# A planned transformer block on one core: w1 in two early loads, block 0's LayerNorm in halves, another order of the first seven products, and turned tokens that go through DRAM

## The chip, the core and the metric

One core of one Trainium2 chip runs the kernel. The core has TensorE (PE; its weight loads are shown as PEld), VectorE (DVE), ScalarE (ACT), GpSimd (POOL) and the queue of SyncE (SP), from which nearly all transfers (DMA) are issued. Each engine works off its own instructions in the order in which they were written, and waits at an instruction until the semaphores that it names have come. The metric is the device time of a run in microseconds (us); the median of the runs of one chip counts.

## The reference

The kernel computes one conditioned block of a sequence model on x of 2 x 2048 x 512 numbers in fp32:

```
emb = silu(t) @ ada_w + ada_b                   # t: 2 x 512, ada_w: 512 x 3072
shift1, scale1, gate1, shift2, scale2, gate2 = split(emb, 6)
norm = layernorm(x) * (1 + scale1) + shift1
h    = gelu(norm @ w1 + b1)                     # w1: 512 x 512
x    = x + gate1 * (h @ w2 + b2)                # w2: 512 x 512
norm = layernorm(x) * (1 + scale2) + shift2
hf   = gelu_tanh(norm @ fw1 + fb1)              # fw1: 512 x 1024
out  = x + gate2 * (hf @ fw2 + fb2)             # fw2: 1024 x 512
```

All numbers are fp32. The six parts of emb are called groups 0 to 5 in the code (mods 0 and 1 are shift1 and scale1, 2 is gate1).

## The kernel before, in words

**Tiling.** The 4096 tokens are eight blocks of 512 (NBLK = 8; four per batch row). A block lies as 128 partitions x 4 slots (C = 4) x 512 features. The work has two stages: for each block `ssm1` (norm @ w1, Gelu) and `ssm2` (h @ w2, added to x; the result x1 is also stored to DRAM), and then, for pairs of blocks, `ff1` and `ff2`. The first stage takes the span's first third, about to 190 us.

**Seven products.** Each matrix product is done with seven half-size products in place of eight (a Strassen form with carried sums): operands are cut in quarters, `first` and `second` (lines 362 and following) form sums of quarters on VectorE and POOL, and P1 to P7 run on TensorE. In `ssm1` a product is four matmuls of 128x256. Products share three banks: P1, P6, P7 and P4 write bank y, P2 bank x, P5 and P3 bank v. In the order CARRIED (P1, P5, P6, P2, P7, P3, P4) ScalarE copies P1's bank to bank x, so that P2 adds to it; P6 adds to P1 in bank y and is taken out by two ScalarE activations (Identity with bias), after which P7 goes on in the same bank. P2's result gets a Gelu, the first one of the kernel, ahead of which the compiler places a table load on ScalarE.

**Turning tokens.** A product needs features on partitions. For block i from 2 on, `norm1` (L562) loads x, takes the statistics on VectorE (`stats`), the scale on POOL (`scales`), normalizes on ScalarE and transposes squares of 32x32 on VectorE (L530) into one of two block buffers (`blocks`, in the tile far). `move` (L556) then brings sixteen pieces of 32 partitions x 512 (64 KB) to their partitions in the tile turned, one transfer each; ScalarE applies shift and scale (`modulate`), and VectorE or POOL form the sums. Blocks 0 and 1 are turned by TensorE (`turn_rows`, matmuls with an identity at L296). `norm2` does the same for the second LayerNorm through DRAM: four transfers of 256 KB out (`turned_d`), and four back in `ff1`'s `tokens`.

**The start.** `small_loads` brings biases and the condition on ScalarE's queue. SP's queue holds x of block 0 (two halves), ada_w's groups 0 and 1, w1 and group 2 (1 MB each), and small loads of gate biases (`load_gate_b`, 1 KB each) where the planner puts them. TensorE runs warm-up products with the identity (`warm`), the two modulations (`modulation`: 16 matmuls, a transpose and an add on VectorE), block 0's turning, and then `ssm1(0)`. Of block 0 the statistics, the scale and the normalizing are done for all four slots at once.

**What sets the order.** `Plan` records every operation with its engines, its cost and its latency. `order` gives each a due time from the order of TensorE's matmuls, which is the program's, and `simulate` plays the queues with these costs and writes out the order that comes of it. Of a transfer it knows the issue, a pipe with a rate, and a landing. So a change of a cost or of one operation can move instructions on VectorE, ScalarE, POOL and SP through the whole program. The framework gives transfers eight semaphores in turn, so that a transfer waits for the eighth before it to land; the planner before does not know of this.

Of the kernel before, what the change touches and what calls it, by code (L numbers as in the profile page):

```python
# [16 lines left out]
class Op:  # L17
    __slots__ = ("n", "engs", "fn", "cost", "lat", "shared", "size", "lead", "care", "after", "done", "deps", "succ", "late", "on", "start", "end", "note")


class Plan:
# [9 lines left out]
    RATED, LANDED = 0.5, 4000.0  # L31
    LITTLE = 1 << 15
    AHEAD, SLACK = 2500.0, 150.0

# [29 lines left out]
    def add(self, engs, fn, outs, ins, cost, lat, shared="", size=0, lead=0.0):  # L64
        op = Op()
        op.n, op.engs, op.fn, op.cost, op.lat, op.shared, op.size = len(self.ops), engs, fn, cost, lat, shared, size
        op.deps, op.succ, op.note, op.lead, op.care = set(), [], self.stage, lead, self.care
        op.after, op.done = None, None
# [12 lines left out]
        self.ops.append(op)  # L81
        return op

    def order(self):
# [11 lines left out]
        for _ in range(2):  # L96
            for op in reversed(ops):
                late = due.get(op.n, 1e9)
                for s in op.succ:
                    late = min(late, ops[s].late - (1 + op.care) * (self.HOP + min(op.lat.values()) + op.size / self.RATE))  # L100
                op.late = late
            self.simulate()
            wait = ops[self.anchor].start - due[self.anchor]
            due = {n: t + wait for n, t in due.items()}
        return sorted(ops, key=lambda op: (op.start, op.n))

    def simulate(self):
# [5 lines left out]
        at, pools, found = 0, {e: [] for e in "vags"}, {}  # L113
        done = [False] * len(ops)

# [8 lines left out]
        def choose(e):  # L124
# [23 lines left out]
        while count:  # L148
# [42 lines left out]
def kernel(  # L191
# [110 lines left out]

    def dma(o, a, q="s", lead=0.0, lat=2000.0):
# [4 lines left out]
        plan.add(q, lambda E: E.dma_start(out=o, in_=a), outs, ins, {q: plan.ISSUE}, {q: lat}, size=size, lead=lead)  # L308

    def memset(o, value):  # L310
# [40 lines left out]

    x1_d = [far(f"x1_{i}", P, C, D) for i in range(NBLK)]
    turned_d = {i: far(f"turned_{i}", P, C, D) for i in SOON}
    fw1_d = far("fw1_parts", 7, P, 7, W)
# [66 lines left out]
    def load_x(i, pieces=1, xs=xs):  # L421
        for s in range(pieces):
            c = slice(s * C // pieces, (s + 1) * C // pieces)
            dma(xs[i][:, c], x_blk[i][:, c])

    def load_ada(g):
        dma(ada_t[g], ada_w[:, g * D : (g + 1) * D].rearrange("(k p) n -> p k n", p=P))

# [54 lines left out]

    def stats(xt):
# [8 lines left out]

    def scales(t, mv, v="g"):
        ve, r, e, rstd, nmr = [t[:, 32 + C * n : 32 + C * (n + 1)] for n in range(5)]
        var, mean = mv[:, :, 1], mv[:, :, 0]
        small("g", lambda E: E.tensor_scalar(ve, var, 1.0, EPS, ALU.mult, ALU.add), ve, [var])
        small("g", lambda E: E.tensor_tensor(r, ve, half_t, ALU.pow), r, [ve, half_t], 1090)  # L498
        if v == "v":
# [4 lines left out]
        else:  # L504
# [5 lines left out]
            small(v, lambda E: E.tensor_scalar(nmr, nmr, -1.0, None, ALU.mult), nmr, [nmr])  # L510
        return rstd, nmr

# [28 lines left out]

    def norm1_sums(i):
        h = cut(turned[i], "p a (k h r) -> p a k h r", k=KD, h=2)
        lo, hi = h[:, :, :2], h[:, :, 2:]
        q = {"11": lo[:, :, :, 0], "12": lo[:, :, :, 1], "21": hi[:, :, :, 0], "22": hi[:, :, :, 1]}
        return second(q, thirds(turned_s[i]))

# [13 lines left out]

    def norm1(i, queues="s"):  # L562
# [7 lines left out]
    def turn_rows(i, xn, k, bank, e):  # L570
        for c in range(C):
            turn_by_pe(banks[bank][:, c * P : (c + 1) * P], xn[:, c, k * P : (k + 1) * P], ident, c == 0, c == C - 1)
        o = turned[i][:, :, k * P : (k + 1) * P].rearrange("p a (c q) -> p a c q", c=C)
        a = cut(banks[bank], "p (c a q) -> p a c q", c=C, a=C)
        shift, scale = mods[0][:, k, :1], mods[1][:, k, :1]
        if e == "v":
            plan.add(
                "v",
                lambda E: E.tensor_scalar(o, a, scale, shift, ALU.mult, ALU.add),
                [o],  # L580
                [a, scale, shift],
                {"v": 600},
                {"v": 690},
            )
        else:
            act(o, a, AF.Identity, shift, scale)

    def rows_normed(i):
# [9 lines left out]
    def norm2(i):  # L598
        plan.stage = f"norm2 {i}"
        bl = normed(xs[i], xs[i], next_blocks())  # L600
        for a in range(C):
            dma(turned_d[i][:, a].rearrange("(m q) r -> q m r", m=C), bl[a * G : (a + 1) * G])

# [28 lines left out]
    def ssm1(i, ops, wops, hooks={}):  # L632
        plan.stage = f"ssm1 {i}"
# [3 lines left out]
        s1, u2, s5 = lo[:, :, :HT], lo[:, :, HT:], hi[:, :, HT:]  # L637
        for n, p in enumerate(CARRIED):
            product(
# [402 lines left out]
    load_ada(0)  # L1042
    load_ada(1)
    load_w(w1_t, w1)
    load_ada(2)
# [21 lines left out]

    t0, mv0 = stats(xs[0])
    plan.add("v", lambda E: E.tensor_copy(cols_t[:, :ROWS], banks[1][:, :ROWS]), [cols_t[:, :ROWS]], [banks[1][:, :ROWS]], {"v": 130}, {"v": 200})
# [9 lines left out]
    plan.add("v", lambda E: E.tensor_copy(picks, pick), [picks], [ident], {"v": 560}, {"v": 640})  # L1079
    rstd0, nmr0 = scales(t0, mv0, "v")  # L1080
    w1q = {"11": w1_t[:, :2, : D // 2], "12": w1_t[:, 2:, : D // 2], "21": w1_t[:, :2, D // 2 :], "22": w1_t[:, 2:, D // 2 :]}
    modulation(0, 1)
    warm((7,) * 3, 2)
    xn = cut(blocks[1], "p (c d) -> p c d", c=C)
    for c in range(C):
        normal(xn, xs[0], c, rstd0, nmr0, "av"[c % 2])
    modulation(1, 2)
# [8 lines left out]
    def turn_first():  # L1096
        plan.stage = "norm1 1"
        for k in range(2):
            turn_rows(1, xn1, k, 1 + k, "a")

    def turn_second():
        plan.stage = "norm1 1"
        for k in range(2, 4):
            turn_rows(1, xn1, k, k - 1, "a")
        tok[1] = norm1_sums(1)
# [4 lines left out]
    plan.anchor = len(plan.ops)  # L1110
    hid = {0: ssm1(0, tok[0], w1_ops, {"P2": lambda: gate_rows_of(2, 1), "P3": first_weight2})}
    w2_ops = gated[0]
# [88 lines left out]
```

## Time and profile before

| what | us |
|---|---|
| median of three runs (579.44, 579.64, 582.99) | 579.64 |
| the profiled execution | 580.96 |
| its span, first to last instruction | 579.2 |
| TensorE busy in the span | 567.2 |
| VectorE, ScalarE, POOL busy | 462.2, 240.2, 319.0 |

The mean granted clock of TensorE is 0.996. In a row of a timeline the columns are start, length, engine, line, operation, tile written and tiles read, shapes, count; in brackets the idle time ahead of it and what ended it. Names ending in q (SPq) are a queue's issue of a transfer. The busy time of TensorE is modelled at the ends of matmuls. Buffer numbers are left out: far, for one, holds block buffers, block 0's x and the identity.

### The profile page before, as it was taken

What the parts mean: (1) busy time and instruction counts of PE and PEld (TensorE: products, weight loads), DVE (VectorE), ACT (ScalarE), POOL (GpSimd) and SP (SyncE); (2) the same over time, 40 slices, a digit from 0 to 9 for tenths busy, and PEclk for the clock granted to TensorE, in tenths of its full rate; (3) what the DMA queues carried; (4) which work ended last, traced back from release to release, by engine and by line L of the source; (5) the groups of instructions that cost most, each with busy time, mean ns of one, the idle gap of its engine ahead of it and who ended that gap; (6) DMA issues with size and microseconds to landing.
All of it is one profiled execution on the core that took longest, in us unless ns stands there. A gap on an engine that the chain in (4) does not pass through costs nothing.

```text
span 579.2 us, 9609 instructions
## 1 busy us (share of the span) xinstructions
PE 567.2 (98%) x3307; PEld 505.6 (87%) x3307; DVE 462.2 (80%) x872; ACT 240.2 (41%) x414; POOL 319.0 (55%) x404
## 2 busy tenths in 40 slices
PE   8999999999998999999999999999999999999997
PEld 5788888888787888888999888999888999888997
DVE  5695865889696688889896789888889997789846
ACT  2463955656384644665202265102255211235010
POOL 1695344889680598976810436711897544336620
PEclk9999999999999999999999999999999999999999
DMA  8953576789578995895034755056846043520022
GB/s 299 392 220 80 185 197 186 220 309 321 175 245 229 346 358 183 314 308 172 30 118 144 236 162 194 23 142 230 296 158 218 1 145 115 195 91 1 2 74 72
DMA packets 49867, 106.96 MB, mean 185 GB/s; under 512 B 6000, under 2 KB 10012, under 8 KB 48924
## 3 DMA queue, kind: packets, MB, share of 16 engines
q1 hardware_dynamic: 49744, 106.34, 55.8%
q8 instruction: 26, 0.43, 0.3%
q14 instruction: 21, 0.17, 0.1%
q10 hardware_dynamic: 76, 0.02, 0.0%
HBM read 68.45 MB, written 31.60 MB: 173 GB/s over the span
## 4 chain that ended last, share of the span: by engine, by line
PE 85%; DMA 5%; POOL 3%; DVE 2%; SPq 2%; issue 1%; ACT 1%; DVEq 0%; ACTq 0%; POOLq 0%
PE bank L286 84%; SPq L308 2%; DMA turned<-far 2%; DMA fw<-in_L_cond_ada_w_dram 1%; DMA ring<-in_L_cond_ssm_w_dram 1%; DMA fw_parts<-fw 1%; POOL near L248 1%; POOL hidden L248 1%; DVE far L530 1%; ACT turned L266 1%; DVE turned L248 0%; POOL fw L248 0%; ACT hidden L266 0%; POOL marks L498 0%; ACT bank L275 0%
## 5 line engine op out<-in xcount | busy, mean ns | idle before, releaser
L286 PE MATMUL bank<-turned,ring 128*128 128x256 f32 x896 | 206.0, 381 | 1.6 <-DMA ring<-in_L_cond_ssm_w_dram 1.3
L286 PEld LDWEIGHTS bank<-turned,ring 128*128 128x128 f32 x896 | 170.2, 191 | 26.3 <-ACT turned L266 1.5
L248 DVE TENSOR_TENSOR hidden<-bank,hidden 128x512 f32<-128x512 f32 (+2 forms) x170 | 125.0, 757 | 41.1 <-PE bank L286 37.4
L248 DVE TENSOR_TENSOR rows<-bank,rows 128x256 f32<-128x256 f32 (+3 forms) x234 | 99.1, 456 | 26.3 <-PE bank L286 19.8
L286 PE MATMUL bank<-near,hidden 128*128 128x256 f32 x448 | 99.9, 382 | 3.8 <-DVE far L248 2.1
L286 PEld LDWEIGHTS bank<-near,hidden 128*128 128x128 f32 x448 | 84.6, 190 | 17.1 <-DVE far L248 2.5
L286 PE MATMUL bank<-ring 128*128 128x256 f32 x336 | 82.2, 381 | 0.0
L286 PE MATMUL bank<-fw,hidden 128*128 128x128 f32 (+1 forms) x512 | 80.1, 301 | 0.0
L286 PEld LDWEIGHTS bank<-fw,hidden 128*128 128x128 f32 x512 | 72.9, 191 | 3.9
L275 ACT COPY bank<-bank 128x512 f32<-128x512 f32 (+2 forms) x67 | 32.3, 482 | 101.4 <-PE bank L286 100.8
L286 PEld LDWEIGHTS bank<-ring 128*128 128x128 f32 x336 | 63.2, 190 | 10.6 <-ACT bank L275 0.8
L248 POOL TENSOR_TENSOR fw<-fw 128x256 f32<-128x256 f32 (+1 forms) x59 | 53.7, 929 | 28.4 <-DMA fw_parts<-fw 12.3
L286 PE MATMUL bank<-fw,far 128*128 128x128 f32 (+2 forms) x624 | 65.8, 286 | 0.3 <-DMA fw<-in_L_cond_ada_w_dram 0.3
L248 POOL TENSOR_TENSOR turned<-turned 128x512 f32<-128x512 f32 (+1 forms) x40 | 45.0, 1140 | 37.9 <-ACT turned L266 17.0
L286 PEld LDWEIGHTS bank<-fw,far 128*128 128x128 f32 (+1 forms) x624 | 59.8, 166 | 3.2 <-issue 1.0
L286 PE MATMUL bank<-fw,near 128*128 128x128 f32 (+1 forms) x432 | 59.5, 290 | 0.0
L286 PEld LDWEIGHTS bank<-fw,near 128*128 128x128 f32 x432 | 54.9, 192 | 1.4
L266 ACT ACTIVATE hidden<-hidden,cols 128x512 f32<-128x512 f32 x64 | 42.6, 714 | 29.3 <-DVE hidden L248 29.1
L266 ACT ACTIVATE turned<-turned,mod,mod 128x512 f32<-128x512 f32 x56 | 41.9, 804 | 21.6 <-DMA turned<-far 10.6
L248 POOL TENSOR_TENSOR hidden<-hidden 128x512 f32<-128x512 f32 (+1 forms) x33 | 40.9, 1243 | 7.1 <-DVE near L248 5.7
L248 POOL TENSOR_TENSOR ring<-turned,ring 128x256 f32<-128x256 f32 x39 | 28.4, 735 | 20.2 <-PE bank L286 13.0
L248 DVE TENSOR_TENSOR turned<-turned 128x512 f32<-128x512 f32 (+1 forms) x52 | 32.2, 642 | 7.3 <-DMA turned<-far 3.9
(102 smaller groups left out, 543.8 us busy)
## 6 DMA issues: line engine op xcount, KB each, us to landing
ring<-fw_parts SPq DMA_DIRECT2D x28, 512.0 KB
ring<-fw_parts SPq DMA_DIRECT2D x28, 384.0 KB, 3.1
turned<-far SPq DMA_DIRECT2D x32, 256.0 KB, 6.1
turned<-turned SPq DMA_DIRECT2D x32, 256.0 KB, 5.9
rows<-x SPq DMA_DIRECT2D x32, 256.0 KB, 4.7
out_dram<-rows SPq DMA_DIRECT2D x30, 256.0 KB, 2.8
fw<-in_L_cond_ada_w_dram SPq DMA_DIRECT2D x6, 1024.0 KB, 11.2
turned<-far SPq DMA_DIRECT2D x96, 64.0 KB, 2.0
```

What stands on the lines that cost most here:

```text
L248: lambda E: E.tensor_tensor(o, a, b, f),
L266: lambda E: E.activation(o, a, func, bias=bias, scale=scale),
L275: plan.add("a", lambda E: E.copy(o, a), [o], [a], {"a": cost}, {"a": cost + 60})
L286: lambda E: E.matmul(o, lhsT, rhs, start=start, stop=stop, skip_group_check=True, **kw),
L308: plan.add(q, lambda E: E.dma_start(out=o, in_=a), outs, ins, {q: plan.ISSUE}, {q: lat}, size=size, lead=lead)
L530: plan.add("v", lambda E: E.transpose(o, a), [o], [a], {"v": 636}, {"v": 705})
```

## The change

1. **w1 and the small loads.** w1 is loaded in two halves (features 0 to 255 and 256 to 511) of 512 KB, and ada_w's group 1 in two halves too. The gate biases get a lead (they are issued at most 12 us ahead of their due time); in SP's order they stand behind w1. The first load of x gets a due time that is 1 us sooner.
2. **Block 0's LayerNorm in halves.** Statistics, scales, normalizing, turning and modulating run for slots 0 and 1 and then for slots 2 and 3. In TensorE's order: the first modulation, two warm-up matmuls (three before), eight transposes of the first half, the second modulation, eight transposes of the second half.
3. **Order FRESH in `ssm1(0)`**: P1, P2, P5, P6, P7, P3, P4. P1 is copied to SBUF (s1) and not to bank x; P2 starts a bank of its own; VectorE adds the two (a new instruction), and the Gelu reads the sum. In ScalarE's order the table load now stands behind the activations of P5, and behind it P2's two Gelus and then P6's two activations.
4. **Turned tokens of blocks 3 to 7** go by `turned_out`: four transfers of 256 KB from the block buffer to a DRAM tensor, and one of 1 MB back into the tile turned, which waits for all four. Block 2 keeps its sixteen.
5. **The planner** knows the eight places for transfers (LANES). Its order of VectorE, ScalarE, POOL and SP differs from the start to the end. TensorE's order is the same from the fifth product of `ssm1(0)` on.

The core of the diff:

```diff
+    LANES = 8
...
+        lanes = [0.0] * self.LANES
...
-                at[op.n] = max(free[e], ready[op.n], wait)
+                at[op.n] = max(free[e], ready[op.n], wait, lanes[0] if op.size else 0.0)
...
+            if op.size:
+                lanes = lanes[1:] + [op.end]
+                found.pop("a", None), found.pop("s", None)
...
+    def turned_out(to, bl):
+        for a in range(C):
+            dma(to[:, a].rearrange("(m q) r -> q m r", m=C), bl[a * G : (a + 1) * G])
...
-        move(turned[i], normed(xs[i], turned[i], next_blocks()), queues)
+        bl = normed(xs[i], turned[i], next_blocks())
+        if i in turned1_d:
+            turned_out(turned1_d[i], bl)
+            dma(turned[i], turned1_d[i])
+        else:
+            move(turned[i], bl)
...
+    FRESH = ("P1", "P2", "P5", "P6", "P7", "P3", "P4")
...
-                p in ("P1", "P5"),
+                p in ("P1", "P5") or p == "P2" and order is FRESH,
...
-                copy(xb, y)
+                copy(xb if order is CARRIED else s1, y)
...
+                if order is FRESH:
+                    tt("v", s1, xb, s1, ALU.add)
                 for j in range(2):
-                    act(s1[:, j], xb[:, j], AF.Gelu, b1T[:, j : j + 1])
+                    act(s1[:, j], (xb if order is CARRIED else s1)[:, j], AF.Gelu, b1T[:, j : j + 1])
...
+                lead=12000.0,
...
-    load_ada(1)
-    load_w(w1_t, w1)
+    load_ada(1, 2)
+    for k in range(0, KD, 2):
+        dma(w1_t[:, k : k + 2], w1[k * P : (k + 2) * P, :].rearrange("(k p) n -> p k n", p=P))
...
+    def normed_half(h):
+        t, mv = stats(xs[0], range(2 * h, 2 * h + 2))
+        rstd, nmr = scales(t, mv, "v", slice(2 * h, 2 * h + 2))
+        for c in (2 * h, 2 * h + 1):
+            normal(xn, xs[0], c, rstd, nmr, "va"[c % 2])
...
     modulation(0, 1)
-    warm((7,) * 3, 2)
-    xn = cut(blocks[1], "p (c d) -> p c d", c=C)
-    for c in range(C):
-        normal(xn, xs[0], c, rstd0, nmr0, "av"[c % 2])
+    warm((7,) * 2, 2)
+    turn_in(0, (0, 3))
     modulation(1, 2)
-    for k in range(KD):
-        turn_rows(0, xn, k, (5, 7, 1, 2)[k], "av"[k % 2])
+    turn_out(0, (0, 3))
+    normed_half(1)
+    turn_in(1, (4, 6))
+    turn_out(1, (4, 6))
```

More of the change, by code (lines that the diff above doesn't have):

```diff
@@ L17 @@
 class Op:
-    __slots__ = ("n", "engs", "fn", "cost", "lat", "shared", "size", "lead", "care", "after", "done", "deps", "succ", "late", "on", "start", "end", "note")
+    __slots__ = ("n", "engs", "fn", "cost", "lat", "shared", "size", "lead", "care", "after", "done", "sooner", "deps", "succ", "late", "on", "start", "end", "note")
 class Plan:
@@ L67, in add @@
         op.deps, op.succ, op.note, op.lead, op.care = set(), [], self.stage, lead, self.care
-        op.after, op.done = None, None
+        op.after, op.done, op.sooner = None, None, 0.0
         for ap in ins:
@@ L100, in order @@
                     late = min(late, ops[s].late - (1 + op.care) * (self.HOP + min(op.lat.values()) + op.size / self.RATE))
-                op.late = late
+                op.late = late - op.sooner
             self.simulate()
@@ L301, in turn_by_pe, with dma @@
         )
[L303 removed]
+    def dma(o, a, q="s", lead=0.0, lat=2000.0, sooner=0.0):
         size = max(cols(o.unsqueeze(0)), 1) * 4
@@ L352 @@
     x1_d = [far(f"x1_{i}", P, C, D) for i in range(NBLK)]
+    turned1_d = {i: far(f"turned1_{i}", P, C, D) for i in range(3, NBLK)}
     turned_d = {i: far(f"turned_{i}", P, C, D) for i in SOON}
@@ L423, in load_x, with load_ada @@
             c = slice(s * C // pieces, (s + 1) * C // pieces)
-            dma(xs[i][:, c], x_blk[i][:, c])
-    def load_ada(g):
-        dma(ada_t[g], ada_w[:, g * D : (g + 1) * D].rearrange("(k p) n -> p k n", p=P))
+            dma(xs[i][:, c], x_blk[i][:, c], sooner=1000.0 * (pieces - 1))
+    def load_ada(g, pieces=1):
+        n = KD // pieces
+        for k in range(0, KD, n):
+            dma(ada_t[g][:, k : k + n], ada_w[k * P : (k + n) * P, g * D : (g + 1) * D].rearrange("(k p) n -> p k n", p=P))
     def load_w(t, w, lead=0.0):
@@ L482, with stats @@
     norms = [0]
-    def stats(xt):
+    def stats(xt, slots=range(C)):
         t = marks[norms[0] % 4]
@@ L492, in stats, with scales @@
         return t, mv
-    def scales(t, mv, v="g"):
-        ve, r, e, rstd, nmr = [t[:, 32 + C * n : 32 + C * (n + 1)] for n in range(5)]
-        var, mean = mv[:, :, 1], mv[:, :, 0]
+    def scales(t, mv, v="g", slots=slice(0, C)):
+        full = [t[:, 32 + C * n : 32 + C * (n + 1)] for n in range(5)]
+        ve, r, e, rstd, nmr = [a[:, slots] for a in full]
+        var, mean, half = mv[:, slots, 1], mv[:, slots, 0], half_t[:, slots]
         small("g", lambda E: E.tensor_scalar(ve, var, 1.0, EPS, ALU.mult, ALU.add), ve, [var])
-        small("g", lambda E: E.tensor_tensor(r, ve, half_t, ALU.pow), r, [ve, half_t], 1090)
+        small("g", lambda E: E.tensor_tensor(r, ve, half, ALU.pow), r, [ve, half], 1090)
         if v == "v":
@@ L568, in norm1, with turn_rows_in, turn_rows_out @@
         return norm1_sums(i)
[L570 to L574, printed above, removed]
+    def turn_rows_in(xn, k, to, slots=range(C), ends=(True, True)):
+        for c in slots:
+            at = (c - slots[0]) * P
+            turn_by_pe(to[:, at : at + P], xn[:, c, k * P : (k + 1) * P], ident, c == slots[0] and ends[0], c == slots[-1] and ends[1])
+    def turn_rows_out(i, k, to, e, slots=range(C)):
+        n = len(slots)
+        o = turned[i][:, :, k * P : (k + 1) * P].rearrange("p a (c q) -> p a c q", c=C)[:, :, slots[0] : slots[0] + n]
+        a = cut(to, "p (c a q) -> p a c q", c=n, a=C)
         shift, scale = mods[0][:, k, :1], mods[1][:, k, :1]
         if e == "v":
+            cost = 128.0 * n / 0.96 + 70
             plan.add(
@@ L581, in turn_rows @@
                 [a, scale, shift],
-                {"v": 600},
-                {"v": 690},
+                {"v": cost},
+                {"v": cost + 90},
             )
@@ L599, in norm2 @@
         plan.stage = f"norm2 {i}"
-        bl = normed(xs[i], xs[i], next_blocks())
-        for a in range(C):
-            dma(turned_d[i][:, a].rearrange("(m q) r -> q m r", m=C), bl[a * G : (a + 1) * G])
+        turned_out(turned_d[i], normed(xs[i], xs[i], next_blocks()))
     stages = [0]
@@ L630, in between, with ssm1 @@
             plan.stage = stage
-    def ssm1(i, ops, wops, hooks={}):
+    def ssm1(i, ops, wops, hooks={}, order=CARRIED):
         plan.stage = f"ssm1 {i}"
@@ L637, in ssm1 @@
         s1, u2, s5 = lo[:, :, :HT], lo[:, :, HT:], hi[:, :, HT:]
-        for n, p in enumerate(CARRIED):
+        for p in order:
             product(
@@ L1066, with turn_in, turn_out @@
     warm((7,), 1)
-    t0, mv0 = stats(xs[0])
+    xn = cut(blocks[0], "p (c d) -> p c d", c=C)
+    def normed_half(h):
[3 more added lines that the diff above has]
+            normal(xn, xs[0], c, rstd, nmr, "va"[c % 2])
+    def turn_in(h, on):
+        for bank, k0 in zip(on, (0, 2)):
+            for k in (k0, k0 + 1):
+                turn_rows_in(xn, k, banks[bank][:, k % 2 * W : (k % 2 + 1) * W], range(2 * h, 2 * h + 2), (k == k0, k > k0))
+    def turn_out(h, on):
+        for k in range(KD):
+            to = banks[on[k // 2]][:, k % 2 * W : (k % 2 + 1) * W]
+            turn_rows_out(0, k, to, "va"[k % 2], range(2 * h, 2 * h + 2))
+    normed_half(0)
     plan.add("v", lambda E: E.tensor_copy(cols_t[:, :ROWS], banks[1][:, :ROWS]), [cols_t[:, :ROWS]], [banks[1][:, :ROWS]], {"v": 130}, {"v": 200})
@@ L1098, in turn_first @@
         for k in range(2):
-            turn_rows(1, xn1, k, 1 + k, "a")
+            turn_rows(1, xn1, k, banks[1 + k], "a")
     def turn_second():
@@ L1103, in turn_second @@
         for k in range(2, 4):
-            turn_rows(1, xn1, k, k - 1, "a")
+            turn_rows(1, xn1, k, banks[k - 1], "a")
         tok[1] = norm1_sums(1)
```

25 lines of the change are left out of this document (14 added, 11 removed).

## The prediction

> **What bounds the kernel now.** I read the page's first part, then who waits for whom on TensorE, then the timeline of each engine around each of those waits.
>
> ```profile
> span 579.2 us, 9609 instructions
> PE 567.2 (98%) x3307; PEld 505.6 (87%) x3307; DVE 462.2 (80%) x872; ACT 240.2 (41%) x414; POOL 319.0 (55%) x404
> ```
> ```profile
> PE bank L286 <- DVE far L248: 2.1, 1, 2.1
> PE bank L286 <- ACT bank L275: 1.6, 2, 1.2
> PE bank L286 <- POOL far masks.py:199: 1.3, 1, 1.3
> PE bank L286 <- DMA ring<-in_L_cond_ssm_w_dram: 1.3, 1, 1.3
> PE bank L296 <- DMA fw<-in_L_cond_ssm_b_dram: 0.8, 1, 0.8
> PE bank L286 <- POOL near L248: 0.4, 1, 0.4
> PE bank L286 <- DMA fw<-in_L_cond_ada_w_dram: 0.3, 1, 0.3
> ```
> TensorE is busy for 98% of the span, and the second list (us in total, times, longest) holds every wait of it: 7.8 us, on the whole run. The change removes no product, so it can only win from those waits and from the work ahead of the first product. Where they lie:
>
> ```profile
> 10.30 1.56 PE L286 MATMUL bank<-far 128*128 128x256 f32 x6
> 11.82 1.08 PE L286 MATMUL bank<-fw,far 128*32 128x128 f32 x32
> 12.84 1.97 PE L296 MATMUL bank<-far 128*128 128x128 f32 x16
> 16.06 7.14 PE L286 MATMUL bank<-turned,ring 128*128 128x256 f32 x32 [1.26 <-DMA ring<-in_L_cond_ssm_w_dram]
> 23.14 1.08 PE L286 MATMUL bank<-fw,far 128*32 128x128 f32 x32
> 24.15 3.72 PE L286 MATMUL bank<-turned,ring 128*128 128x256 f32 x16
> ...
> 35.29 3.72 PE L286 MATMUL bank<-near,hidden 128*128 128x256 f32 x16 [0.39 <-POOL near L248]
> ...
> 88.38 8.87 PE L286 MATMUL bank<-turned,ring 128*128 128x256 f32 x40 [0.31 <-ACT bank L275]
> ...
> 150.85 8.87 PE L286 MATMUL bank<-near,hidden 128*128 128x256 f32 x40 [1.24 <-ACT bank L275]
> ...
> 184.27 2.55 PE L286 MATMUL bank<-near,hidden 128*128 128x256 f32 x8 [2.10 <-DVE far L248]
> ```
> The reader is to see two things: block 0's first four products run in 16.06 to 23.14 (1.785 us each) after a wait for w1; and the stream loses 0.39, 0.31, 1.24 and 2.10 us later (4.04 together), nothing after 184.27. The last three have their roots in these rows of VectorE and ScalarE:
>
> ```profile
> 83.46 2.49 DVE L530 STREAM_TRANSPOSE far<-turned 128x512 f32<-128x512 f32 x4 [1.57 <-DMA turned<-far]
> ...
> 146.09 1.29 DVE L490 BATCH_NORM_STATS2 marks<-rows 128x6 f32<-128x512 f32 x2 [2.25 <-DMA rows<-in_x_dram]
> ...
> 181.72 1.89 DVE L248 TENSOR_TENSOR turned<-turned 128x512 f32<-128x512 f32 x3 [3.93 <-DMA turned<-far]
> ```
> ```profile
> 178.70 2.93 ACT L266 ACTIVATE turned<-turned,mod,mod 128x512 f32<-128x512 f32 x4 [3.79 <-DMA turned<-far]
> ```
> Each time an instruction that needs a transfer stands in VectorE's queue ahead of the adds that empty TensorE's banks. Two of the three transfers are the sixteen small ones of a turned block; the third (146.09) is a load of x, which the change leaves as it is.
>
> **The start, step by step.** Rows of SP's queue and of the transfers:
>
> ```profile
> 4.83 0.40 SPq L308 DMA_DIRECT2D fw<-in_L_cond_ada_w_dram  x1
> ...
> 9.17 0.39 SPq L308 DMA_DIRECT2D ring<-in_L_cond_ssm_w_dram  x1
> ```
> ```profile
> 1.64 7.51 DMA fw<-in_L_cond_ada_w_dram
> ```
> ```profile
> 0.00:8.10 8.10, 5.92 (x10) 2.51 (x11) 3.73 (x8) 1.58 (x3) 1.51 (x11) 1.00 0.73 258
> 8.10:9.20 1.10, 0.91 (x4) 0.38 (x2) 0.82 (x5) 0.12 (x1) 0.23 (x2) 1.00 1.05 406
> ```
> w1 was issued at 9.17, just after the first ada_w load had landed (1.64 + 7.51 = 9.15): in this program each transfer waits for the eighth before it, and the small gate rows had used up places. Now the gate rows stand behind w1, and its halves wait only for the first half of x, as the ada_w load at 4.83 does in this trace, and for a small load from ScalarE's queue: issued at about 5. The transfers run in order, and 8.10 x 258 = 2090 KB, x and the first ada_w, had moved at 8.1 for a landing at 9.15 (1.05 later). x, two ada_w and w1 are 4194 KB; at 406 KB per us from 9.2 (2537 KB) that is 13.3, so w1's second half lands at about 14.3 and the first, 524 KB earlier, at 13.0. The four x and ada loads before them do not move.
>
> So the LayerNorm decides the start. Its first half runs beside the ada loads at no cost. But half of the turning now stands in TensorE's queue ahead of the second modulation: two warm products in place of three, 10.30 + 2/3 x 1.56 = 11.34; eight transposes, half of 1.97, to 12.3; the modulation 1.08, to 13.4, where it ended at 12.90.
>
> ```profile
> 13.34 0.17 DVE L452 TENSOR_TENSOR mod<-bank,cols 128x8 f32<-128x8 f32 x1
> 13.97 1.68 DVE L579 TENSOR_SCALAR turned<-bank,mod,mod 128x512 f32<-128x512 f32 x2 [0.46 <-PE bank L296]
> ```
> ```profile
> 13.60 1.58 ACT L266 ACTIVATE turned<-bank,mod,mod 128x512 f32<-128x512 f32 x2 [0.95 <-DVE mod L452]
> ...
> 19.79 0.84 ACT L266 ACTIVATE hidden<-bank,cols 128x256 f32<-128x256 f32 x2 [1.16 <-PE bank L286]
> ...
> 23.29 1.28 ACT L266 ACT_TABLE_LOAD   x1 [0.93 <-PE bank L286]
> ...
> 234.72 0.57 ACT L275 COPY bank<-bank 128x512 f32<-128x512 f32 x1 [1.20 <-PE bank L286]
> 235.31 1.28 ACT L266 ACT_TABLE_LOAD   x1
> ```
> Both scale vectors are then ready at 13.51 + 0.5 = 14.0. VectorE's half tile costs half of 0.84, so P1 starts at 14.5, and its second product waits for ScalarE's half (between 0.40 and 0.79, I take 0.5, and it stands behind VectorE's) until 15.05. P1 therefore ends as if it had started at 14.65, 1.4 us ahead of 16.06, and w1 (13.0, 14.3) holds neither P1 nor P2 (16.4).
>
> Most of this is given back at the fifth product. In the new order P6 is the fourth product and P7, which writes the same bank, the fifth; P7 must wait until ScalarE has copied P6 out, and in ScalarE's new order the table load and P2's two Gelus stand ahead of that copy. Before, the copy of P6 (the third product) lay ahead of the table load, which cost nothing because P7's bank was free. Counted: P5 ends at 14.65 + 3 x 1.785 = 20.0; its copy begins 0.16 later and takes 0.84, to 21.0; the table load 1.28, to 22.3; two Gelus and two copies of 128x256, 2 x 0.84 less 0.1 of overlap, to 23.9. P7 starts at 23.95. It could have started at 22.8 (14.65 + 7.14 + the modulation's 1.0); before it started at 24.15. The start so wins **0.2 us**, not 1.4. Bounds: 1.4 if the load were hidden, and 0 if P1 waits for w1 as now. P2's new add on VectorE lies beside P6 and the load.
>
> [...]
>
> **The rest.** *The 0.39 at 35.29*: the sums of w2 hang on POOL behind the gate, which follows P3; they come as much earlier as P7, and POOL's order has one sum of hidden ahead of them that is ready sooner. I take 0.25 of 0.39 (0 to 0.39).
>
> *Turned blocks 3 to 7.* Removed: 16 transfers of 64 KB; added: four of 256 KB out and one of 1 MB back, so eleven issues fewer in each of five blocks.
>
> ```profile
> 163.31 12.15 SPq L308 DMA_DIRECT2D turned<-far  x16
> ...
> 176.19 3.58 SPq L308 DMA_DIRECT2D turned<-far  x4
> ```
> ```profile
> turned<-far SPq DMA_DIRECT2D x32, 256.0 KB, 6.1
> ...
> rows<-in_x_dram SPq DMA_DIRECT2D x3, 1024.0 KB, 9.4
> ring<-in_x_dram SPq DMA_DIRECT2D x2, 1024.0 KB, 5.0
> ```
> Old way: 163.31 to 178.70, 15.4 us from the first issue to the modulation. New way: the four issues as in 176.19 (3.58), 6.1 to landing, 0.5 for the next issue, then 5.0 to 9.4 for 1 MB: 15.2 to 19.6. No block gets its tokens sooner by this. What it wins is elsewhere: the block buffer is free after 3.58 + 6.1 = 9.7 us and not after some 15, and SP is free for 8.6 us more (12.15 less 3.58) per block. What waits at 83.46 is the buffer, so the 0.31 goes. At 181.72 block 7's tokens came late because its transposes did: VectorE had fallen behind with block 6, and SP sent that block's sixteen transfers ahead of much else. In the changed order nothing of the kind lies ahead of block 7's transposes, and from the add behind which the last of them stands to the add behind which the sum of its tokens stands TensorE has fourteen products, 14 x 1.785 = 25 us. The trip with the modulation (2.93) takes 18.1 to 22.5. It fits, so I take the 2.10 as gone (0 to 2.10). The 1.24 stays: the x load behind it is issued as late as before, into the same queue. Queued on SP behind its new wait (the read waits for the four writes to land) are mostly the stores of fw1's sums, whose first readers are the ring loads after 184, and once block 0's second turning, whose buffer is next needed some six products later; I charge nothing, with one wait of the size seen, 2.1, as the upper bound.
>
> *The planner's lanes and the other due times* reorder VectorE, POOL and SP to the end. TensorE's order after the start is unchanged, and it waited nowhere after 184.27 at the old order; I charge 0, bounded by the same 2.1.
>
> **Sum**: 0.2 + 0.25 + 0.31 + 2.10 = 2.86 us. The profiled execution took 580.96 (span 579.2), 1.32 over the median of 579.64: 578.1 by its own time, and against the median 576.8.
>
> **Rivals.**
> *The start wins what it looks like* (1.4 in place of 0.2), and the x load is in time as well (1.24): 574.4. For it: w1 is out of the way by my own count. Against: the load's place in ScalarE's order is fixed. 0.15.
> *It doesn't do what it says*: the round trip takes the long end in the crowded blocks and gives back in new waits what it saves, 2.7 in all: 579.5. For it: 6.1 and 9.4 are medians, so half of such transfers land later. 0.15.
> *Slower*: in block 7 the read lands 4.2 us later than the sixteen did (19.6 against 15.4) and TensorE has as little room as in this trace. Then 2.10 is not won and 4.2 is lost, less the 0.76 of the other terms: +3.4, 583.1. It decides from 0.8 us later than now, 16.2 us for the trip. Against: the room of 25 us counted above. 0.12.
> [...] 0.05.
>
> **How the numbers follow.** The forecast, 575.5 to 578, has 0.53; with the rivals 1. Likeliest: 576.8. The range 574.2 to 580.6 takes in the first two rivals and the fourth; left out are the slower one and a tail below. About 1% is what a measurement of this kernel tells from no change, so faster means below 573.8 (only if every wait goes and the load hides: 0.04), slower above 585.4 (the slower rival in two blocks: 0.04), and the same 0.92.
>
> **What would show it.** Right: first product at about 14.5, the table load between the copy and the Gelus at about 21, P7 at about 24 with TensorE idle before it for some 1.1 us behind ScalarE; no wait of TensorE near 88 or 182, one near 149; five reads of 1 MB into the turned tiles landing in 5 to 9 us. Wrong: P7 near 22.8, or VectorE waiting for those reads with TensorE's banks full.

## The result, and the profile after

The changed kernel takes 574.79 us in the median of four runs (574.67 to 575.45), the kernel before 581.32 in four runs beside it (579.44 to 583.38): a ratio of 0.9912, 95% interval 0.9885 to 0.9938. Five rounds beside three of the experiments gave 575.09 against 579.97 and 0.9913 (0.9886 to 0.9939). So it is faster by 0.9%, just under the 1% that the prediction took as the least to be called faster. By the medians 5 to 6.5 us are won, and 6.2 us between the two profiled executions (spans 579.2 and 573.0). The prediction was 576.8, with 2.86 us won.

TensorE's waits in the profile after (us in total, times, longest) come to 4.3 us, where there were 7.8:

```profile
PE bank L290 <- POOL half L317: 1.3, 1, 1.3
PE bank L290 <- POOL turned L252: 1.2, 1, 1.2
PE bank L300 <- DMA fw<-in_L_cond_ssm_b_dram: 1.1, 1, 1.1
PE bank L290 <- POOL near L252: 0.5, 2, 0.3
PE bank L290 <- DVE turned L604: 0.2, 1, 0.2
```

The timeline of TensorE after; the rows answer to those shown of before:

```profile
13.18 1.09 PE L300 MATMUL bank<-far 128*128 128x128 f32 x8
14.48 7.40 PE L290 MATMUL bank<-turned,ring 128*128 128x256 f32 x32 [0.21 <-DVE turned L604]
21.81 1.08 PE L290 MATMUL bank<-fw,far 128*32 128x128 f32 x32
24.12 3.69 PE L290 MATMUL bank<-turned,ring 128*128 128x256 f32 x16 [1.23 <-POOL turned L252]
...
35.10 3.07 PE L290 MATMUL bank<-near,hidden 128*128 128x256 f32 x13 [0.26 <-POOL near L252]
...
84.69 10.52 PE L290 MATMUL bank<-turned,ring 128*128 128x256 f32 x48
...
144.69 7.50 PE L290 MATMUL bank<-near,hidden 128*128 128x256 f32 x34
...
180.96 12.25 PE L290 MATMUL bank<-turned,ring 128*128 128x256 f32 x56
...
432.91 1.97 PE L290 MATMUL bank<-turned,ring 128*128 128x256 f32 x8 [0.27 <-POOL near L252]
```

The reader is to see that the first product starts 1.6 us sooner (14.48 against 16.06) and the fifth hardly sooner (24.12 against 24.15), and that the stream then runs without a break over the places of the three later waits.

Following the start of the same matmul through both traces gives a ledger. The lead of the changed kernel is 0.03 us at the fifth product, 0.19 at 46.7, 0.74 behind the place of the wait at 88, 1.29 at 108 (some matmuls of before between 103 and 108 start 0.1 to 0.2 late each), 2.77 behind 150, 5.65 at 180.96 (the row that is 186.61 in before), 6.83 at 182.3, and 6.27 at the end, after a new wait at 432. With the wider spacing of the matmuls right behind each, the waits at 88 and 150 are so worth 0.55 and 1.48. Of the 2.88 up to 180.96, the wait at 184 is worth 2.47; the other 0.41 are two matmuls behind it, and with the 1.18 that follow 1.6 us are won where no wait is: the lead grows by 0.21 with each matmul there. The windows of before there (length, busy time of each engine, then the granted clock of TensorE, the DMA share and GB/s):

```profile
181.50:184.30 2.80, 0.70 (x5) 0.27 (x3) 2.58 (x5) 1.54 (x3) 0.07 (x1) 1.00 0.74 174
184.30:185.60 1.30, 1.30 (x6) 1.17 (x7) 1.30 (x3) 0.00 (x0) 0.00 (x0) 0.99 0.87 271
185.60:189.00 3.40, 3.40 (x10) 2.69 (x9) 3.38 (x6) 1.15 (x2) 0.00 (x0) 0.50 0.94 309
```

TensorE is busy there at a granted clock of 0.50, from 185.57 to 188.98. The trace after has no such stretch ahead of its last matmul (1.00 from the start to 570).

ScalarE at the start of the changed kernel:

```profile
20.19 0.84 ACT L270 ACTIVATE hidden<-bank,cols 128x256 f32<-128x256 f32 x2 [2.55 <-PE bank L290]
21.05 1.28 ACT L270 ACT_TABLE_LOAD   x1
22.34 0.91 ACT L270 ACTIVATE hidden<-hidden,cols 128x256 f32<-128x256 f32 x2
23.16 0.82 ACT L270 ACTIVATE hidden<-bank,cols 128x256 f32<-128x256 f32 x2
```

The copy of P5, the load, P2's Gelus, and only then the copy of P6 out of the bank that P7 needs: it ends at 23.98, and P7 starts at 24.12.

### The profile page after: what moved, and what is told of

Same layout as the page of the kernel before. It is cut to its first block, busy times and chain, and to the rows that moved or that the text cites. A ratio compares the mean times of both kernels' runs of the same rounds, so it can differ in the third digit from the quotient of the medians.

```text
span 573.0 us, 9505 instructions
## 1 busy us (share of the span) xinstructions
PE 564.3 (98%) x3305; PEld 504.5 (88%) x3305; DVE 471.9 (82%) x891; ACT 240.7 (42%) x416; POOL 302.5 (53%) x394
## 4 chain that ended last, share of the span: by engine, by line
PE 92%; POOL 3%; DVE 2%; DMA 1%; issue 1%; ACT 1%; ACTq 0%; DVEq 0%; POOLq 0%
PE bank L290 92%; POOL fw L252 1%; DMA fw<-in_L_cond_ssm_b_dram 1%; DVE hidden L252 1%; POOL ring L252 1%; DVE turned L252 1%; POOL near L252 1%; PE bank L300 0%; DVE fw L252 0%; ACT turned L270 0%; DVE turned L604 0%; POOL hidden L252 0%; POOL turned L252 0%; ACTq L312 0%; DVE rows L252 0%
## 5 line engine op out<-in xcount | busy, mean ns | idle before, releaser
L290 PE MATMUL bank<-near,hidden 128*128 128x256 f32 x448 | 98.4, 380 | 0.3 <-POOL near L252 0.3
L252 POOL TENSOR_TENSOR fw<-fw 128x256 f32<-128x256 f32 (+1 forms) x63 | 57.9, 939 | 12.9 <-DVE fw L252 7.7
L270 ACT ACTIVATE hidden<-hidden,cols 128x512 f32<-128x512 f32 (+1 forms) x66 | 43.1, 707 | 24.5 <-DVE hidden L252 24.3
L270 ACT ACTIVATE turned<-turned,mod,mod 128x512 f32<-128x512 f32 x56 | 42.0, 805 | 15.5 <-DMA turned<-turned 15.4
L252 POOL TENSOR_TENSOR turned<-turned 128x512 f32<-128x512 f32 (+1 forms) x35 | 38.5, 1115 | 13.9 <-ACT turned L270 8.9
L252 POOL TENSOR_TENSOR hidden<-hidden 128x512 f32<-128x512 f32 (+1 forms) x26 | 32.5, 1254 | 22.2 <-ACT hidden L270 17.1
L252 DVE TENSOR_TENSOR turned<-turned 128x512 f32<-128x512 f32 (+1 forms) x57 | 35.6, 656 | 3.8 <-ACT turned L270 3.0
```

Of the source, the lines that this page charges most:

```text
L252: lambda E: E.tensor_tensor(o, a, b, f),
L270: lambda E: E.activation(o, a, func, bias=bias, scale=scale),
L290: lambda E: E.matmul(o, lhsT, rhs, start=start, stop=stop, skip_group_check=True, **kw),
```

## The experiments

Times are medians, ratios go against the kernel before, in runs beside it on the same chip. "The changed kernel" stands for 574.79 and 575.09.

**The table load.** One tiny Gelu is added where ScalarE idles; the compiler puts the load ahead of it.

```diff
     turn_in(1, (4, 6))
+    plan.add("a", lambda E: E.activation(marks[1][:, 52:56], xn[:, 3, :C], AF.Gelu), [marks[1][:, 52:56]], [xn[:, 3, :C]], {"a": 1500}, {"a": 1500})
     turn_out(1, (4, 6))
```

> The changed kernel with one tiny Gelu (128x4, into an unused corner) on ScalarE behind the second half's normalizing, where ScalarE is idle from 12.0 to 14.5: the table load then stands there and not at 21.05 between the activations of the fifth and the second product; nothing else moves on any engine. Theory (the load holds P6's copy out and so P7): no load at 21, P6's copies end near 22.7, P7 starts at 22.8 to 22.95 in place of 24.12 with TensorE idle under 0.2 us before it, time 573.4 to 573.9. Rival 1 (P7 waits for a sum of w1 on GpSimd, as the profile's list of waits puts it down): P7 stays at 24.1, 574.8. Rival 2 (the 1.2 us is given back at the next wait, since GpSimd's sums of w2 come no sooner): P7 at 22.9 but a wait of about 1 us before ssm2's products near 34 to 35, time 574.5 to 574.9.

> The kernel with the early table load once more, for its time and a profile in which the first transfers land as usual: 573.3 to 573.9; P7 at 22.8 to 22.95 when the first product starts at 14.5, ScalarE's copies of P6 ended by 22.7. Rival as before: P7 at 24.1.

573.61 us, ratio 0.9891 (0.9873 to 0.9910), and once more 573.57, ratio 0.9913 (0.9884 to 0.9941). In the first profile a small load on ScalarE's queue came late and the whole start lay 1.1 us later; the second shows the start as usual, ScalarE, then TensorE, then one row of GpSimd:

```profile
11.87 1.28 ACT L1139 ACT_TABLE_LOAD   x1
...
20.16 0.84 ACT L270 ACTIVATE hidden<-bank,cols 128x256 f32<-128x256 f32 x2 [2.54 <-PE bank L290]
20.90 0.91 ACT L270 ACTIVATE hidden<-hidden,cols 128x256 f32<-128x256 f32 x2
21.88 0.84 ACT L270 ACTIVATE hidden<-bank,cols 128x256 f32<-128x256 f32 x2
```
```profile
14.45 7.40 PE L290 MATMUL bank<-turned,ring 128*128 128x256 f32 x32 [0.21 <-DVE turned L604]
21.77 1.08 PE L290 MATMUL bank<-fw,far 128*32 128x128 f32 x32
22.87 3.69 PE L290 MATMUL bank<-turned,ring 128*128 128x256 f32 x16
...
33.85 3.72 PE L290 MATMUL bank<-near,hidden 128*128 128x256 f32 x16 [0.26 <-POOL near L252]
```
```profile
22.81 1.27 POOL L252 TENSOR_TENSOR turned<-turned 128x512 f32<-128x512 f32 x1
```

P7 starts at 22.87 and the 1.25 us stay won. The load held it, as predicted. The profile had put that wait down to a GpSimd sum ("POOL turned"); in this run that sum goes on to 24.08 and P7 doesn't wait for it. This is the fastest kernel here by the medians.

**The start of before in the changed kernel.** Undone are points 1 to 3 of the change (the early loads and their leads, the LayerNorm's halves, the order FRESH); the route through DRAM and the planner's lanes stay. Three places of the diff:

```diff
-    for k in range(0, KD, 2):
-        dma(w1_t[:, k : k + 2], w1[k * P : (k + 2) * P, :].rearrange("(k p) n -> p k n", p=P))
+    load_w(w1_t, w1)
...
-    normed_half(0)
+    t0, mv0 = stats(xs[0])
...
-    hid = {0: ssm1(0, tok[0], w1_ops, {"P6": lambda: gate_rows_of(2, 1), "P3": first_weight2}, FRESH)}
+    hid = {0: ssm1(0, tok[0], w1_ops, {"P2": lambda: gate_rows_of(2, 1), "P3": first_weight2})}
```

> The changed kernel with the start of before (w1 in one load behind the gate rows, the LayerNorm in one piece, order P1 P5 P6 P2 P7); the lanes and the route through DRAM stay. Theory (the start wins 0.2 and the wait at 35 about 0.1, the rest is the route): first product at 15.5 to 16.1, fifth at 23.5 to 24.2, time 574.8 to 575.8. Rival (the earlier start is worth what it looks like, 1.4 to 1.6 us): 576.2 to 576.6. If the planner's lanes alone bring w1 ahead of the gate rows, the first product starts at about 14.9 with the old LayerNorm, the fifth at 23.0, and this kernel is faster than the changed one: 573.6 to 574.2.

577.28 us, ratio 0.9944 (0.9922 to 0.9967). Block 0 did what the last sentence allowed for: the lanes alone bring w1 forward, the first product starts at 14.59 and the fifth at 22.98, 1.1 us ahead of the changed kernel. Yet the time is 2.2 to 2.5 longer; the profile, its shortest run, shows a new wait near 181:

```profile
181.72 4.64 PE L290 MATMUL bank<-turned,ring 128*128 128x256 f32 x19 [1.11 <-ACT turned L270]
```
```profile
180.85 2.93 ACT L270 ACTIVATE turned<-turned,mod,mod 128x512 f32<-128x512 f32 x4 [0.53 <-DMA turned<-turned]
```

That is block 7's read of 1 MB (issued at 172.83): ScalarE gets it at 180.85, and TensorE goes on 0.05 us after the first quarter is modulated (181.67).

Either the new start has a worth that shows late, or the planner's other order behind block 0 costs it. The next kernel tells: the same start, with the place of every later instruction of VectorE, ScalarE, GpSimd and SP written out as the changed kernel has it (a few instructions of the first 40 us still go with block 0). The line that does it, without the table of places:

```diff
-    for op in plan.order():
+    for op in plan.order() and kept_order(plan, special):
```

> The start of before (LayerNorm in one piece, order P1 P5 P6 P2 P7, w1 in one load) as in the kernel with the old start, but every queue (VectorE, ScalarE, GpSimd, SP) behind block 0 keeps the order of the changed kernel, written out by hand in place of the planner's. Theory (in the kernel with the old start the planner's other order behind block 0 cost the time, and the start itself was ahead: fifth product at 22.98 against 24.12): fifth product at 22.9 to 23.1 again, no wait of TensorE over 0.5 us between 30 and 190, time 573.4 to 574.2, below the changed kernel. Rival (the new start has a worth that shows only later, the order has little to do with it): 576 to 578 as with the old start.

574.42 us (the changed kernel beside it 575.09), ratio 0.9900 (0.9873 to 0.9927). TensorE:

```profile
14.56 7.43 PE L290 MATMUL bank<-turned,ring 128*128 128x256 f32 x32
21.92 1.08 PE L290 MATMUL bank<-fw,far 128*32 128x128 f32 x32
22.93 3.72 PE L290 MATMUL bank<-turned,ring 128*128 128x256 f32 x16
...
34.57 3.72 PE L290 MATMUL bank<-near,hidden 128*128 128x256 f32 x16 [0.50 <-POOL near L252]
```

No other wait over 0.2 lies between 25 and 190. So the order cost the 2.9 us between the two medians; the two profiles show 1.15 of it, and where the rest lies no trace shows. The old start, with w1 in time, beats the new one by 0.7; the rest of its lead of 1.2 is lost between 31 and 35, at the sums of w2.

**The halves with the old order of products**, later queues kept as above.

```diff
-    hid = {0: ssm1(0, tok[0], w1_ops, {"P6": lambda: gate_rows_of(2, 1), "P3": first_weight2}, FRESH)}
+    hid = {0: ssm1(0, tok[0], w1_ops, {"P2": lambda: gate_rows_of(2, 1), "P3": first_weight2})}
```

> The changed kernel (w1 early, LayerNorm in halves) with the old order of products P1 P5 P6 P2 P7 in block 0; the queues behind block 0 keep the changed kernel's order. Theory (the halves push block 0's token sums back, the modulating ends at 17.2 and the first sum at 18.2, so that the order FRESH is needed with the halves, and costs 1.2 at P7 by the table load): the second product, now P5, waits until about 18.2 to 18.4, 1.9 to 2.2 us idle; P7 starts at 24.7 to 25.0; time 575.2 to 576.2. Rival (the halves alone are harmless, FRESH alone costs): no wait over 0.3 before P5, P7 at 22.9 to 23.0, time 573.6 to 574.2.

574.42 us, ratio 0.9928 (0.9902 to 0.9954).

```profile
14.62 7.63 PE L290 MATMUL bank<-turned,ring 128*128 128x256 f32 x32 [0.20 <-DVE turned L607]
22.18 1.08 PE L290 MATMUL bank<-fw,far 128*32 128x128 f32 x32
23.19 3.72 PE L290 MATMUL bank<-turned,ring 128*128 128x256 f32 x16
```

My theory fell. P5 has its sums in time, since the modulating now ends at 15.9 on VectorE and 16.6 on ScalarE, not at 17.2; the first four products lose some 0.2 us in all. FRESH isn't needed with the halves, and without it the wait is gone.

**Sixteen transfers again for blocks 3 to 7**, first in the planner's own order.

```diff
-    turned1_d = {i: far(f"turned1_{i}", P, C, D) for i in range(3, NBLK)}
+    turned1_d = {i: far(f"turned1_{i}", P, C, D) for i in ()}
```

> The changed kernel with blocks 3 to 7 turned by sixteen 64 KB transfers again; the new start and the planner's lanes stay. Theory (the route through DRAM removes the waits of TensorE at about 88, 150 and 184, since it frees the block buffer and SP's queue): these waits come back in whole or in part, at least one of over 1 us between 140 and 190, and the time is 577.5 to 581, i.e. 3 to 6 us above the changed kernel's 574.8; TensorE's first product still starts at 14.5. Rival 1 (the planner's lanes alone reorder the queues so that the waits go): within 0.6 us of 574.8 and no wait over 0.5 us after 25 us. Rival 2 (the half-speed stretch of TensorE's clock of before, 185.6 to 189.0, follows from the 2.1 us wait): if a wait over 1 us comes back here, a stretch of granted clock 0.5 stands behind it too; if there is such a stretch without a wait, or a wait without it, that rival falls.

578.07 us, ratio 0.9963 (0.9945 to 0.9981). The waits come back elsewhere, at 100.03 and 193.46, none between 140 and 190:

```profile
PE bank L290 <- ACT bank L279: 1.7, 1, 1.7
PE bank L290 <- POOL marks L515: 1.6, 1, 1.6
```

My theory had named a wait of over 1 us between 140 and 190; its time came, its place did not. No stretch at half clock follows either of the two (1.00 from 99 to 106 and from 192 to 200). Block 7's x is issued at 147.89 here, later than in the kernel before, and TensorE doesn't wait for it, since VectorE takes its statistics at 154.49 only, with other adds ahead of them. Then the same edit with the order of all other instructions kept, so that only the transfers of these blocks differ. The sixteen stand where the four writes stood:

```diff
-    for op in plan.order():
+    for op in plan.order() and kept_order(plan, special):
```

> The changed kernel with the sixteen 64 KB transfers in place of the five for blocks 3 to 7, all other instructions of every engine and of SP in the changed kernel's order. Theory (the route itself does it: SP's queue is held some 8 us longer per block and the block buffer comes free later): waits of over 1 us in all come back between 60 and 190, time 576.5 to 579. Rival (the planner's order did it, the route only gave it other costs to plan with): within 0.6 us of the changed kernel, 574.3 to 575.5.

593.55 us, ratio 1.0238 (1.0204 to 1.0273): much more than either theory said. SP, VectorE and TensorE of this run:

```profile
138.40 10.01 SPq L312 DMA_DIRECT2D turned<-far  x16
148.51 0.53 SPq L312 DMA_DIRECT2D rows<-in_x_dram  x1
```
```profile
140.16 0.70 DVE L539 STREAM_TRANSPOSE far<-rows 128x512 f32<-128x512 f32 x1
...
155.08 1.29 DVE L498 BATCH_NORM_STATS2 marks<-rows 128x6 f32<-128x512 f32 x2 [7.86 <-DMA rows<-in_x_dram]
```
```profile
157.32 2.90 PE L290 MATMUL bank<-turned,ring 128*128 128x256 f32 x6 [7.92 <-DVE hidden L252]
```

The load of block 7's x could go from 140.9 on, when the last transpose of its place ends, but stands in SP's queue behind block 6's sixteen issues; VectorE stands still at the statistics, with the adds that empty TensorE's banks behind them. That is the wait of before at 150 in kind, 24 matmuls earlier and enlarged. From 152.12 on, within this stop, the granted clock is 0.50 for 10.24 us (the run's mean is 0.991).

**The changed kernel once more**, as it is, beside the kernels with the kept order and the one with stops below.

> The changed kernel unchanged, on the same chip as the three others, for the comparison: 574.3 to 575.3, and waits of TensorE as in its first profile.

575.09 us, as told above; its profile has the same 1.2 us wait at P7 and none between 40 and 190.

**The planner without lanes.**

```diff
-                lanes = lanes[1:] + [op.end]
+                lanes = lanes[1:] + [0.0]
```

> The changed kernel with the planner blind again to the eight places for transfers; the start and the route through DRAM stay. Theory (the route does the work): 574.3 to 576, the waits at 88 and 184 stay away. Rival (the lanes do it): the waits of before come back, 577.5 or more. In between, 576 to 577.5, would say that the lanes matter for one of the three waits, most likely the one at 150, which hangs on the place of the x load in SP's queue.

576.28 us, ratio 0.9941 (0.9917 to 0.9964). The intervals of this and of the changed kernel overlap; the medians differ by 1.2 to 1.5, between theory and rival. The waits at 88, 150 and 184 stay away, so it isn't the lanes that remove them. Its profile has one new wait in the first stage, 0.4 us at 181, again for block 7's read, which ScalarE gets at 180.67; what else the lanes win no trace shows.

**Stops put into TensorE's stream**, to see whether the half clock belongs to the wait of before.

```diff
+            stop = count >= 620 and (count - 620) % 42 == 0
+            if stop:
+                for n in range((4, 11, 7, 13, 9, 16)[(count - 620) // 42 % 6]):
+                    wait = nc.scalar.activation(idle, half_t[:, :1].to_broadcast([P, 64 - ROWS]), AF.Identity)
...
```

> The changed kernel with some 25 artificial stops of TensorE, one each 42 matmuls behind the 620th: a chain of 4, 11, 7, 13, 9 or 16 tiny ScalarE instructions (128x20, into an unused corner) between one matmul and the next, some 0.8 to 4 us long. Theory (TensorE's clock is granted by windows of about 3.4 us; a stop that fills more than about half of one halves the clock for the next): no stretch of granted clock 0.5 behind stops under 1.6 us, behind every stop of 3.4 us or more, and behind some of those between 1.7 and 3.4, each stretch 3.4 us long and costing 1.7. Rival (the stretch in the profile of before came by chance, or from something other than the wait): stretches without relation to the stops' lengths, or none.

670.23 us, with a mean granted clock of 0.958 in the profiled execution. Of 25 stops 12 are followed by half clock (0.50), and length alone doesn't tell which. Two stops and the time behind each:

```profile
352.80:356.01 3.21, 0.00 (x1) 0.03 (x1) 0.69 (x1) 2.89 (x13) 0.00 (x0) 1.00 0.41 150
356.01:360.00 3.99, 3.99 (x19) 3.52 (x20) 2.66 (x6) 2.21 (x4) 0.95 (x2) 1.00 0.00 0
512.55:514.92 2.37, 0.00 (x1) 0.01 (x1) 0.34 (x1) 1.96 (x9) 0.00 (x0) 1.00 0.00 0
515.17:518.58 3.41, 3.41 (x18) 3.41 (x18) 1.74 (x4) 0.00 (x0) 1.18 (x1) 0.50 0.00 0
```

Behind the stop of 3.21 us the clock stays at 1.00, behind the one of 2.37 it is 0.50. In this trace the starts of all half-clock stretches lie whole multiples of 3.413 us apart (those at 515.17 and 532.23, for two, by five); a window is here one step of that grid. On it the stop of 3.21 us is cut into 0.57 and 0.37 of two windows, and the one of 2.37 lies in one and fills 0.69 of it. So it goes for all 25: the 13 with no half clock behind them fill at most 0.57 of any window, the 12 others at least 0.59 of one. Eight of the stretches last one window (3.41 us) and four last two (6.83), which I had not expected; the four are those whose stop runs on into the next window for 0.30 of it or more. By its own grid, the stop of before (182.16 to 184.27) filled 0.62. The stop of 7.92 us in the kernel with the kept order filled 0.80, 1.00 and 0.52 of three windows, and three windows from the end of the first on are at half clock; the two waits with the sixteen transfers in the planner's order filled at most 0.47.

## Why the prediction was right, and where it was not

574.79 lies below the forecast of 575.5 to 578 and within the range of 574.2 to 580.6, which reached so low only because it took in a rival at 574.4. That the time came out in the range is in part luck: of the terms below three were in the sum, and the other gains were not.

*The start: right in its mechanism and its times.* w1 issued at 4.77, its sums on GpSimd from 14.68, second modulation ended at 13.25 (13.4), first product 14.48 (14.5), load 21.05 (21.0), copy of P6 done 23.98 (23.9), P7 24.12 (23.95). With the wait at 35 it won 0.19, where 0.45 stood: P7 0.17 later than reckoned, and the 0.39 only went to 0.26. What I left out is that the price is optional: w1 in time with the old order of products puts P7 at 22.93 to 23.19.

*The table load costs its own 1.28 us.* The load starts 0.02 us after the copy ahead of it and the Gelu 0.01 after the load (21.05 + 1.28 = 22.33); in before, too, the load at 235.31 starts 0.02 after a copy ends. With the load at 11.87, P7 came 1.25 us sooner (22.87 against 24.12). The fourth rival, at 0.05, reckoned with a longer switch, and no run shows one.

*88 and 184: both went, and the cause is in part argued.* Block 7's tokens made the trip by the long end: the first of its four transfers goes out at 158.38, its read is the third of the five rows at 168.21 (issued at 170.21), and ScalarE gets it at 177.83:

```profile
158.38 4.08 SPq L312 DMA_DIRECT2D turned<-far  x4
...
168.21 3.54 SPq L312 DMA_DIRECT2D turned<-turned  x5
```
```profile
177.83 2.93 ACT L270 ACTIVATE turned<-turned,mod,mod 128x512 f32<-128x512 f32 x4 [6.47 <-DMA turned<-turned]
```

19.45 us, of 15.2 to 19.6 reckoned and against 15.4 before. TensorE doesn't wait, but little of the room was left: its first product of block 7 starts at 180.96, and the first quarter is modulated at 178.64. In the kernels without lanes and with the old start the read came some 3 us later and TensorE waited for it, 0.4 and 1.1 us at 181, as in the rival "slower", on a smaller scale. The five reads landed in 7.7 us in the median, of 5 to 9 foreseen. The route wins nothing in the trip, as the prediction said. That it wins by freeing SP's queue and the block buffer fits the kernel with the kept order: there the sixteen issues hold up the load of x, and at 193.33 VectorE waits 3.13 us for a block buffer that is still being read, and TensorE 1.83 behind it, sixteen matmuls ahead of the place of 184. That it removed just these two waits no run shows: with the sixteen transfers back, in either order, no wait stands at their two matmuls.

*150: the step that failed.* "The 1.24 stays: the x load behind it is issued as late as before, into the same queue." It was issued at 132.67, not 136.62 (SP before and after), because it waits for the last transpose of the block in whose place it lands. In before that transpose ends at 135.32 + 1.28 = 136.60, after at 131.95 + 0.69 = 132.64.

```profile
136.62 0.33 SPq L308 DMA_DIRECT2D rows<-in_x_dram  x1
```
```profile
132.67 0.35 SPq L312 DMA_DIRECT2D rows<-in_x_dram  x1
```

First before, then after, on VectorE:

```profile
135.32 1.28 DVE L530 STREAM_TRANSPOSE far<-rows 128x512 f32<-128x512 f32 x2
```
```profile
131.95 0.69 DVE L539 STREAM_TRANSPOSE far<-rows 128x512 f32<-128x512 f32 x1
...
139.21 1.29 DVE L498 BATCH_NORM_STATS2 marks<-rows 128x6 f32<-128x512 f32 x2 [0.21 <-DMA rows<-in_x_dram]
```

VectorE waits 0.21 for it where it waited 2.25, and 1.48 us are won. The earlier issue alone doesn't explain it: VectorE also comes to the statistics 4.84 us sooner (139.00 against 143.84), and the issue is 3.95 sooner. The load also took 6.5 us from issue to landing in place of 9.4, so "into the same queue" failed too. I had looked at the place of the transfer and not at what frees its target, nor at what else is under way. Without lanes and with the old start the load is still early (132.90 and 132.10); with sixteen issues ahead of it, it comes late (147.89 and 148.51), and then VectorE's order decides whether TensorE waits. Why the planner now places these transposes earlier, and why the load was quicker, no run takes apart further.

*The half clock: not seen.* 1.6 us of the gain between the two profiles. The windows of before showed it (0.50 from 185.6 on), but I had taken a wait to cost its own length. Of the 40 executions of the kernel before beside the experiments 11 have a mean clock of 0.997 or less, as the profiled one has (0.996), and a median of 581.56; the other 29 have 578.99. So most executions of before seem to be without the stretch, and the medians' 5 us hold little of it.

*The order of the rest: charged at 0, within a bound of 2.1.* The small late starts at 103 to 108 went (0.55), and 0.56 was lost behind 182, most of it at the new wait at 432. Other variants go beyond the bound: the order alone is worth 2.9 us between the two kernels with the old start, and with the kept order the sixteen transfers cost 18.5 us where in their own they cost 3. So the parts have no fixed prices here. Undone one at a time in the planner's order they cost 3.1 (route), 2.3 (start) and 1.3 (lanes) by the medians, 6.7 together where the whole is worth 5; the intervals of the last two overlap with that of the changed kernel.

The sum, in order of time (the start, 88, 103 to 108, 150, 184, the half clock, behind 182): 0.19 + 0.55 + 0.55 + 1.48 + 2.47 + 1.6 - 0.56 = 6.28 of span, where 2.86 was predicted. The prediction had 0.45 for the first term, 0.31 for the second and 2.10 for the fifth, and nothing for the others. Without the half clock it is 4.7, near the 5 of the medians. The execution profiled before (580.96) had the half-clock stretch and lies 1.0 over the median of its kernel beside the experiments (579.95); the medians differ by 5. Of the rivals, "the start wins 1.4 and the x load is in time" named the time best (574.4), but only its second half happened.

## What to carry to other kernels

Before pricing an edit that reorders products, look what the new order puts between a bank and the engine that empties it: here a table load of 1.28 us, and one tiny activation at an idle place removed it. Ask of a late transfer what frees its target and where its reader stands, not only which queue it stands in. And where a planner writes the order, test a part with the rest of the order held fixed, or its price is that of another schedule.

## What the runs showed of the hardware

In the kernel with the 25 stops the half-clock stretches of TensorE (0.50) began whole multiples of 3.413 us apart. The 12 stops that filled 0.59 or more of one such window had half clock behind them, for one window, or for two where the stop ran on into the next for 0.30 of it or more; the 13 that filled at most 0.57 had none. In the kernel before, the stop of 2.11 us filled 0.62, and one window (3.41 us) at 0.50 followed, in which 1.6 us were lost. By an estimate from these two runs a wait of 2.1 us costs either 2.1 or some 3.7 us (2.1 + 1.6), by where it falls on the grid.
